# Reordering the row pieces of a DFT stage so that rows loaded from DRAM lie beside a chain of small operations and its exponentials

## Chip, core, metric

One NeuronCore of one Trainium2 chip runs the whole program. The metric is device time in microseconds (us) of one execution; the time before is the median of three runs. Times on the page and in the trace are in us from the first instruction, unless ns is written.

Names of engines: PE is TensorE (matrix multiply), PEld its weight loads, DVE is VectorE, ACT is ScalarE, POOL is GpSimd, and SP is the engine that issues the DMAs.

## What is computed

The input is `x` of shape (8, 256, 96, 96): eight images of 256 channels. Two layers, each with a group norm ahead of it and a residual around it:

```python
# layer 0: attention over channels in the Fourier domain
q_f = fft2(pconv(gn(x), w1, b1)); k_f = fft2(pconv(gn(x), w2, b2)); v_f = fft2(pconv(gn(x), w3, b3))
q_f = l2_normalize(q_f); k_f = l2_normalize(k_f)             # over all 9216 positions, 8 heads of 32 channels
attn = einsum('bhcn,bhdn->bhcd', q_f, k_f) * temperature
attn = softmax(real(attn)) + 1j * softmax(imag(attn))
x = x + pconv(abs(ifft2(einsum('bhcd,bhdn->bhcn', attn, v_f))), w_out)
# layer 1: linear attention with softplus features
x = x + L1_conv(gn(x), Wq, bq, Wk, bk, Wv, bv)
```

The kernel never transforms the images for q and k: it needs only channel sums of products (`pair_sums`), from which the 32 x 32 logits of each head follow. The values need one more linear map of every image along its rows and columns. That map is "R" of the change: `rotate(b)` multiplies each row of image b, transposed, by a table of its own.

## The kernel before: the stage that the change touches

For each image b the program runs, one after the other: `attention(b)` woven with `rotate(b)`; the rest of `rotate(b)`; `images(b)`; `layer1(b)`; `output(b)`. The channel sums of the next image are woven into the last three.

`rotate(b)` is a generator of 48 steps. A step handles two rows h and h+1 of the image. For rows that are not spilled it transposes them on PE (four 128 x 128 transposes), and ACT copies the result from PSUM into a ring of six slots, `xT`. Rows 16 to 79 but for 48 are "spilled" in images 1 to 7: `pair_sums` has already written them, transposed, to DRAM (`xtd`), and a DMA of 192 KB brings the two rows into the slot instead. Two steps later the rows are multiplied by their table (`tm`), and the product is copied from PSUM to the image `y`.

```python
def spilled(h):
    return b > 0 and PR * T0 <= h < H - PR * T0 and h != H // 2       # 16 <= h < 80, not 48

pieces = [TR * i for i in (15, 14, 3, 4, 0, 5, 6, 1, 7, 8, 13, 9, 10, 2, 11, 12)]   # TR = 6 rows
order = [h + r for h in pieces for r in range(0, TR, 2)]
...
def fetch(i):
    if i < len(order) and spilled(order[i]):
        xts[i] = xT[:, i % NX]                                        # NX = 6
        ...
        nc.sync.dma_start(out=xts[i][0:W, :, 0:C], in_=rows.rearrange("(r w) n -> w r n", w=W))

def step(h, due, xt=None, on_scalar=False):
    if h is not None:
        pt = ps_tile(f"xr_{b}_{h}")                                   # ps: a pool of five PSUM banks
    if due is not None:
        g, gt, tm = due
        pu = ps_tile(f"y_{b}_{g}")
    for r in range(2):
        for k in range(KC):
            if h is not None and h + r:
                nc.tensor.transpose(pt[...], x_of(b)[:, k, o:o + W], ident)            # L661
            if due is not None and g + r:
                nc.tensor.matmul(pu[...], lhsT=gt[...], rhs=tm[:, g % TR + r, :], ...)  # L664
    if due is not None:
        nc.vector.tensor_copy(ys[:, :, g + r:g + 2], src[:, :, W, r:2])                 # L669
        (nc.scalar.copy if on_scalar else nc.vector.tensor_copy)(y[...], src[...])      # L670
    if h is not None:
        nc.scalar.copy(xt[0:W, r:2, 0:C], pt[...])                                      # L674

tms = [load_r(g) for g in pieces[0:3]]            # tables, three buffers, one load of 218 KB for a piece
...
for i, h in enumerate(order):
    if i % (TR // 2) == 2 and i > 2 and pieces:
        tms.append(load_r(pieces.pop(0)))
    ...
    due = pending.pop(0) if len(pending) == 2 else None
    step(None if spilled(h) else h, due, xts[i],
         due is not None and spilled(due[0]) and spilled(h) and i % 2)
    pending.append((h, xts.pop(i), tm))
    fetch(i + 3)
    yield
```

`attention(b)` is a chain of small operations for the 32 x 32 logits. Each `yield n` in it lets n steps of `rotate` run before the chain goes on:

```python
... group norm ...                       # yields 2, 1
... scr, cov ...                ; yield 4
qkm matmuls                     ; yield 1        # after step 6
covT, scaling by rstd           ; yield 2        # after step 7
cw products, m = 0, 1           ; yield 1, 1     # after steps 9, 10
cw2 matmuls, ACT scales them    ; yield 2        # after step 11
lg logits, m = 0, 1             ; yield 1, 1     # after steps 13, 14
ssk, square roots, reciprocal   ; yield 1        # after step 15
ssq, square roots, reciprocal   ; yield 4        # after step 16
ls = lg * rk * rq, maximum, two Exp on ACT (L556), division, sbd   ; yield 10   # after step 20
at matmuls (L566)               ; yield 3        # after step 30
mz matmuls (L580)               ; yield 1, 1     # after steps 33, 34
```

PE and POOL keep this program order here; the order on DVE and ACT is chosen by the scheduler when the program is built, earlier code first where both are ready.

Of the kernel before, what the change touches and what calls it, by code (L numbers as in the profile page):

```python
# [62 lines left out]
TR = 6  # L63
# [9 lines left out]
def two_layer_kernel(ctx: ExitStack, tc: tile.TileContext, x, w1t, b1, w2t, b2, w3, b3, wot, temp,  # L73
# [26 lines left out]
    def x_of(b):  # L100
        return arenas[b % 2]

    def y_of(b):
        return arenas[1 - b % 2]

    def x_col(h):

        if h < H // 2:
            t, r = divmod(h, PR)
        elif h == H // 2:  # L110
            t, r = 0, 2 * PR - 1
        else:
            t = (H - h) // PR
            r = 2 * PR - 1 - (H - h) % PR
        return ((NT - 1 - t) * ROWS + r) * W
# [14 lines left out]
    def ps_tile(name):  # L130
        return psum.tile([P, 512], F32, tag="ps", name=name)
# [147 lines left out]
    def window(h, n, back):  # L279

        v = (rb if back else rt)[h:h + n, 0 if back else 1:]
        return bass.AP(v.tensor, v.offset, [[1, W], [2 * W, n], [1, W]])

    def turned(c, h, w):

        return xtd[c, (h - PR * T0) * W + w:]
# [36 lines left out]
    def image(t):  # L323
        return t.rearrange("p k (h w) -> p k h w", w=W)
# [282 lines left out]
    def rotate(b):  # L607

        y = image(y_of(b))
        ys = one.tile([P, KC, H + 1], F32, tag="ys", name=f"ys_{b}")  # L610

        def spilled(h):

            return b > 0 and PR * T0 <= h < H - PR * T0 and h != H // 2

        def load_r(h):
            tm = three.tile([P, TR * (W + 1)], F32, tag="tm", name=f"tm_{b}_{h}")[0:W].rearrange("p (r w) -> p r w", r=TR)
            turned = H // 2 <= h < H - PR * T0
            if b > turned:
                nc.sync.dma_start(out=tm, in_=rx[h // TR])  # L620
                return tm
            lo = 0
            while lo < TR:
                back = h + lo > H // 2 and spilled(h + lo)
                hi = lo + 2
                while hi < TR and back == (h + hi > H // 2 and spilled(h + hi)):
                    hi += 2
                nc.sync.dma_start(out=tm[:, lo:hi, 0:W], in_=window(h + lo, hi - lo, back))
                lo = hi
            nc.gpsimd.tensor_copy(tm[:, :, W:W + 1], csn[0:W, 2, h:h + TR].unsqueeze(2))  # L630
            if b == turned:
                nc.sync.dma_start(out=rx[h // TR], in_=tm)
            return tm


        pieces = [TR * i for i in (15, 14, 3, 4, 0, 5, 6, 1, 7, 8, 13, 9, 10, 2, 11, 12)]
        order = [h + r for h in pieces for r in range(0, TR, 2)]
        xts = {}

        def fetch(i):  # L640

            if i < len(order) and spilled(order[i]):
                xts[i] = xT[:, i % NX]
                h = order[i]
                c = h > H // 2
                rows = turned(c, H - h - 1 if c else h, 0)[0:2 * W]
# [5 lines that stand above are left out]
                pt = ps_tile(f"xr_{b}_{h}")  # L652
            if due is not None:
                g, gt, tm = due
                back = g > H // 2 and spilled(g)
# [4 lines that stand above are left out]
                        o = x_col(h + r)  # L660
                        nc.tensor.transpose(pt[0:W, r * C + k * P:r * C + (k + 1) * P], x_of(b)[:, k, o:o + W], ident)  # L661
                    if due is not None and g + r:
                        o = (r * KC + k) * (W + 1)
                        nc.tensor.matmul(pu[:, o:o + W + 1], lhsT=gt[0:W, 1 - r if back else r, k * P:(k + 1) * P], rhs=tm[:, g % TR + r, :],  # L664
                                         start=True, stop=True)
            if due is not None:
                src = pu[:, 0:2 * KC * (W + 1)].rearrange("p (r k w) -> p k w r", r=2, k=KC)
                r = 0 if g else 1
                nc.vector.tensor_copy(ys[:, :, g + r:g + 2], src[:, :, W, r:2])  # L669
                (nc.scalar.copy if on_scalar else nc.vector.tensor_copy)(  # L670
                    y[:, :, :, g + r:g + 2], src[:, :, 0:W, r:2] if back else src[:, :, W - 1::-1, r:2])
            if h is not None:
                r = 0 if h else 1
                nc.scalar.copy(xt[0:W, r:2, 0:C], pt[0:W, r * C:2 * C].rearrange("p (r n) -> p r n", n=C))  # L674

        tms = [load_r(g) for g in pieces[0:3]]
        pieces = pieces[3:]
        pending = []
        for i, h in enumerate(order):
            if i % (TR // 2) == 0:  # L680
                tm = tms.pop(0)
            if i % (TR // 2) == 2 and i > 2 and pieces:
                tms.append(load_r(pieces.pop(0)))
            if i == len(order) - TR:
                o = x_col(0)
                nc.gpsimd.tensor_copy(y[:, :, :, 0], x_of(b)[:, :, o:o + W])
                nc.gpsimd.memset(ys[:, :, 0:1], 0.0)
            if not spilled(h):
                xts[i] = xT[:, i % NX]
            due = pending.pop(0) if len(pending) == 2 else None  # L690
            step(None if spilled(h) else h, due, xts[i], due is not None and spilled(due[0]) and spilled(h) and i % 2)
            pending.append((h, xts.pop(i), tm))
            fetch(i + 3)
            yield
        for p in pending:
            step(None, p)
        y0[b] = ys
# [333 lines left out]
    with tc.manual_schedule(engines={mybir.EngineType.DVE, mybir.EngineType.Pool}):  # L1031
        for _ in range(NT):
            next(sums)
        tables()
        finish(sums)
    turns = rotate(0)
    for b in range(B):
        with tc.manual_schedule(engines={mybir.EngineType.PE, mybir.EngineType.Pool}):
            weave(attention(b), turns)
            finish(turns)  # L1040
            b3_part(b)
        sums = pair_sums(b + 1) if b + 1 < B else iter(())
        weave(images(b), sums)
        weave(layer1(b), sums)
        with tc.manual_schedule(engines={mybir.EngineType.PE, mybir.EngineType.DVE, mybir.EngineType.Pool, mybir.EngineType.SP,
                                         mybir.EngineType.Activation}):
            weave(output(b, *l1.pop(b)), sums)
            if b + 1 < B:
                turns = rotate(b + 1)
                finish(sums)  # L1050
# [50 lines left out]
```

## Time and profile before

| what | before |
|---|---|
| time, median of 3 runs | 2730.31 us |
| lowest, highest run | 2726.63, 2734.25 us |
| span of the profiled execution, mean granted PE clock | 2728.5 us, 0.984 |
| products of rows (L664, PE), in image 2 of eight | 380 matmuls, median 275 ns |
| copies of products, L670: on DVE, on ACT | 321 of 548 ns, 63 of 491 ns (medians) |
| copies of transposed rows, L674 (ACT) | 167, median 583 ns |
| loads of spilled rows, `xT<-xtd` | 217 of 192 KB |
| loads of tables, `tm<-rx` | 106 of 218.2 KB |

How to read it: a matrix multiply in 32-bit floats is counted as two PE instructions. Busy shares are averages over stages with different limits, so the questions are when PE stands still within this stage, what it waits for, and at what clock it goes on. A stage here is the stretch from the first transpose of `rotate(b)` to the first matmul of `images(b)`.

### The profile page before, as it was taken

What the parts mean: (1) busy time and instruction counts of PE and PEld (TensorE: products, weight loads), DVE (VectorE), ACT (ScalarE), POOL (GpSimd) and SP (SyncE); (2) the same over time, 40 slices, a digit from 0 to 9 for tenths busy, and PEclk for the clock granted to TensorE, in tenths of its full rate; (3) what the DMA queues carried; (4) which work ended last, traced back from release to release, by engine and by line L of the source; (5) the groups of instructions that cost most, each with busy time, mean ns of one, the idle gap of its engine ahead of it and who ended that gap; (6) DMA issues with size and microseconds to landing.
All of it is one profiled execution on the core that took longest, in us unless ns stands there. A gap on an engine that the chain in (4) does not pass through costs nothing. (4 is left out here: it accounts for less than half of the span.)

```text
span 2728.5 us, 47701 instructions
## 1 busy us (share of the span) xinstructions
PE 2682.3 (98%) x17494; PEld 1927.4 (71%) x17494; DVE 1922.3 (70%) x4099; ACT 1355.1 (50%) x2160; POOL 890.1 (33%) x1335
## 2 busy tenths in 40 slices
PE   9999999999999999999999999999999999999988
PEld 8965679656786567955679567785677856778546
DVE  6678576785768757587676876768757596576766
ACT  3455653455535565255642556425474355643554
POOL 6133431334313344033440443404424134241311
PEclk9999998999999999999999999999999999999997
DMA  5220265302652026520275203642036410373003
GB/s 175 67 65 12 70 215 166 85 18 65 203 182 78 10 78 233 149 64 10 82 235 143 70 20 99 223 134 58 30 104 225 123 53 32 102 231 100 1 7 139
DMA packets 243183, 283.59 MB, mean 104 GB/s; under 512 B 37380, under 2 KB 231240, under 8 KB 242952
## 3 DMA queue, kind: packets, MB, share of 16 engines
q1 hardware_dynamic: 242008, 280.22, 33.2%
q8 instruction: 140, 2.29, 0.4%
q14 instruction: 91, 0.75, 0.1%
q10 hardware_dynamic: 944, 0.34, 0.0%
HBM read 156.76 MB, written 123.72 MB: 103 GB/s over the span
## 5 line engine op out<-in xcount | busy, mean ns | idle before, releaser
L746 PE MATMUL z<-arena,mz 128*128 128x384 f32 (+2 forms) x2400 | 597.6, 480 | 0.0
L758 PE MATMUL po<-e,wo 128*128 128x384 f32 x1536 | 529.7, 486 | 0.2 <-ACT e L793 0.2
L792 POOL TENSOR_TENSOR e<-e 128x768 f32<-128x768 f32 x192 | 348.6, 1815 | 554.1 <-ACT e L791 550.5
L746 PEld LDWEIGHTS z<-arena,mz 128*128 128x128 f32 (+1 forms) x2400 | 326.3, 164 | 243.5 <-issue 44.5
L337 PE MATMUL acc<-xT 128*128 128x256 f32 (+1 forms) x2368 | 447.4, 330 | 2.5 <-POOL xT L417 1.8
L664 PE MATMUL y<-tm,xT 96*128 96x97 f32 x3040 | 421.8, 277 | 9.2 <-ACT xT L674 6.4
L758 PEld LDWEIGHTS po<-e,wo 128*128 128x128 f32 x1536 | 289.4, 190 | 197.7 <-DVE arena L760 1.2
L664 PEld LDWEIGHTS y<-tm,xT 96*128 96x128 f32 x3040 | 411.6, 198 | 24.8 <-issue 12.9
L787 DVE TENSOR_TENSOR e<-z,xT 128x768 f32<-128x768 f32 x384 | 365.8, 953 | 86.0 <-PE z L746 85.2
L290 DVE BATCH_NORM_STATS2 st<-arena 128x6 f32<-128x384 f32 x768 | 410.2, 553 | 13.2 <-DMA arena<-in_x_dram 2.8
L337 PEld LDWEIGHTS acc<-xT 128*128 128x128 f32 x2368 | 382.0, 191 | 44.8 <-DVE xT L419 5.9
L791 ACT ACTIVATE e<-e 128x1536 f32<-128x1536 f32 x192 | 284.5, 1482 | 91.4 <-DVE e L787 89.9
L793 ACT ACTIVATE e<-e 128x768 f32<-128x768 f32 x192 | 161.9, 843 | 337.2 <-POOL e L792 334.7
L405 ACT ACTIVATE xt<-eoT,pw 128x512 f32<-128x512 f32 x296 | 203.6, 688 | 181.0 <-PE eoT L404 169.3
L417 POOL TENSOR_TENSOR xT<-xt 128x256 f32<-128x256 f32 x352 | 256.9, 747 | 70.8 <-ACT xt L405 69.3
L760 DVE TENSOR_TENSOR arena<-arena,po 128x384 f32<-128x384 f32 x384 | 211.0, 551 | 90.6 <-PE po L758 67.6
L669 DVE COPY ys<-y 128x4 f32<-128x4 f32 (+1 forms) x384 | 62.0, 161 | 182.6 <-PE y L664 181.8
L670 DVE COPY arena<-y 128x384 f32<-128x384 f32 (+1 forms) x321 | 175.2, 546 | 1.4 <-issue 1.4
L674 ACT COPY xT<-xr 96x512 f32<-96x512 f32 (+1 forms) x167 | 94.5, 572 | 156.9 <-PE xr L661 143.0
L381 POOL COPY back<-arena 128x256 f32<-128x256 f32 (+1 forms) x230 | 86.0, 380 | 265.1 <-PE eoT L404 253.9
L1005 POOL TENSOR_TENSOR arena<-arena,po 128x384 f32<-128x384 f32 x96 | 96.4, 1004 | 232.4 <-ACT po L1004 229.5
L661 PE MATMUL xr<-ident,arena 128*96 128x128 f32 x652 | 171.4, 281 | 0.0
(235 smaller groups left out, 3311.1 us busy)
## 6 DMA issues: line engine op xcount, KB each, us to landing
out_dram<-arena SPq DMA_DIRECT2D x184, 384.0 KB
arena<-in_x_dram SPq DMA_DIRECT2D x182, 384.0 KB
xtd<-xt SPq DMA_DIRECT2D x336, 128.0 KB
xT<-xtd SPq DMA_DIRECT2D x217, 192.0 KB
tm<-rx SPq DMA_DIRECT2D x106, 218.2 KB
rx<-tm SPq DMA_DIRECT2D x16, 218.2 KB
tm<-rt SPq DMA_DIRECT2D x16, 216.0 KB
arena<-in_x_dram SPq DMA_DIRECT2D x8, 288.0 KB
```

Source lines behind the costliest of these rows:

```text
L290: nc.vector.bn_stats(out=st[:, k, c, :], in_=x_of(b)[:, k, c * CH:(c + 1) * CH])
L337: mm = nc.tensor.matmul(acc[c][:, m * C:m * C + (KC - m) * P], lhsT=t[0:np_, c, m * P:(m + 1) * P], rhs=t[0:np_, c, m * P:C], start=(first ...
L405: nc.scalar.activation(both, pt, AF.Copy, scale=pw[:, j:j + 1])
L417: on_pool(eo[:, c], both[:, 0], both[:, 1])
L664: nc.tensor.matmul(pu[:, o:o + W + 1], lhsT=gt[0:W, 1 - r if back else r, k * P:(k + 1) * P], rhs=tm[:, g % TR + r, :], start=True, stop=True)
L670: (nc.scalar.copy if on_scalar else nc.vector.tensor_copy)(y[:, :, :, g + r:g + 2], src[:, :, 0:W, r:2] if back else src[:, :, W - 1::-1, ...
L746: mm = nc.tensor.matmul(out[:, o:o + n * W], lhsT=columns(mz, k, c, j), rhs=y[:, k, h * W:(h + n) * W], start=(k == 0 and o == 0), stop=(k ...
L758: nc.tensor.matmul(po[:, 0:CH], lhsT=wo[:, k, m * P:(m + 1) * P], rhs=e[:, k, :], start=(k == 0), stop=(k == KC - 1))
L760: nc.vector.tensor_add(x[:, m, n], x[:, m, n], po[:, 0:CH])
L787: nc.vector.tensor_add(e[:, 2 * c:2 * c + 2, :].rearrange("p t (q h) -> p t q h", h=H), pz[:, 0:CH].rearrange("p (q h) -> p q h", h=H).uns ...
L791: nc.scalar.activation(e, e, AF.Square)
L792: nc.gpsimd.tensor_add(e[:, 0:2, :], e[:, 0:2, :], e[:, 2:4, :])
```

## The change

The pieces of six rows are taken in another order. Rows that come from DRAM need no transposes and no copy by ACT, so steps with such rows are short on PE and leave ACT alone. The change puts twelve such steps in a row (6 to 17) beside the densest part of the chain, six more (21 to 26) beside the exponentials, and spreads the others, which had been bunched at the end, over the rest. It also keeps ACT from copying products in steps 24 to 27.

```diff
-        pieces = [TR * i for i in (15, 14, 3, 4, 0, 5, 6, 1, 7, 8, 13, 9, 10, 2, 11, 12)]
+        pieces = [TR * i for i in (15, 14, 3, 4, 5, 6, 0, 7, 9, 1, 8, 10, 2, 11, 13, 12)]
...
-            step(None if spilled(h) else h, due, xts[i], due is not None and spilled(due[0]) and spilled(h) and i % 2)
+            step(None if spilled(h) else h, due, xts[i], due is not None and spilled(due[0]) and spilled(h) and i % 2 and not 24 <= i < 28)
```

## Prediction

> **What bounds the kernel now.** I read the page first. Its engine totals name the only candidate; the slices below them say that the clock is not always full.
>
> ```profile
> PE 2682.3 (98%) x17494; PEld 1927.4 (71%) x17494; DVE 1922.3 (70%) x4099; ACT 1355.1 (50%) x2160; POOL 890.1 (33%) x1335
> ```
>
> PE has something in its pipe for 98% of the span, so a change of order that adds and removes no matmul can gain in two ways only: PE stands still less, or runs less at a reduced clock. Next I asked what PE waits for.
>
> ```profile
> PE y L664 <- ACT xT L674: 6.4, 8, 0.9
> ...
> PE y L664 <- DMA xT<-xtd: 2.1, 2, 1.4
> ```
>
> Both top lines of this stage are small: 6.4 us in eight waits on ACT's copy of transposed rows, 2.1 us in two waits for a row from DRAM. Then I cut the span into the seven stages of images 1 to 7, each from its first transpose to the first matmul of `images` (columns: length; busy time and instructions of PE, PEld, DVE, ACT, POOL; granted clock; DMA share; GB/s).
>
> ```profile
> 419.07:492.92 73.85, 71.55 (x537) 67.94 (x535) 39.43 (x136) 19.44 (x40) 1.91 (x11) 0.86 0.52 145
> 763.23:826.06 62.83, 61.98 (x538) 58.52 (x536) 39.42 (x136) 19.47 (x40) 0.20 (x2) 1.00 0.50 146
> 1094.67:1162.67 68.00, 67.09 (x537) 63.47 (x535) 39.44 (x136) 19.49 (x40) 0.39 (x4) 0.92 0.47 136
> 1434.28:1497.34 63.06, 62.12 (x538) 58.52 (x536) 39.34 (x136) 19.48 (x40) 0.20 (x2) 1.00 0.52 145
> 1765.79:1829.42 63.63, 62.13 (x538) 58.53 (x536) 39.34 (x136) 19.46 (x40) 0.28 (x4) 1.00 0.51 144
> 2098.03:2166.05 68.02, 67.17 (x537) 63.48 (x535) 39.42 (x136) 19.47 (x40) 0.20 (x2) 0.92 0.48 136
> 2434.53:2497.30 62.77, 61.92 (x537) 58.46 (x535) 39.34 (x136) 19.45 (x40) 0.30 (x4) 1.00 0.52 147
> ```
>
> The same 537 or 538 instructions take 62.8 us at clock 1.00 and 68.0 or 73.9 us at 0.92 and 0.86. Stages that differ in nothing but clock differ by 5 to 11 us. Where does the clock fall? I took the pieces of lower clock from the trace's record of it and put beside them the same work of image 2 (last line).
>
> ```profile
> 455.80:469.50 13.70, 13.70 (x69) 13.68 (x69) 4.87 (x17) 1.24 (x3) 0.45 (x3) 0.50 0.56 149
> 486.50:496.80 10.30, 10.30 (x79) 9.26 (x81) 2.95 (x13) 0.48 (x1) 0.16 (x2) 0.50 0.05 15
> 1131.70:1141.90 10.20, 10.20 (x51) 10.18 (x51) 3.95 (x14) 0.58 (x1) 0.00 (x0) 0.50 0.42 123
> 2135.20:2145.40 10.20, 10.20 (x51) 10.18 (x50) 3.94 (x14) 0.58 (x1) 0.00 (x0) 0.50 0.41 121
> 798.90:809.10 10.20, 10.20 (x93) 10.07 (x91) 6.80 (x24) 1.75 (x3) 0.00 (x0) 1.00 0.62 187
> ```
>
> At clock 0.50 a stretch of 10.2 us holds 51 matmuls, at 1.00 it holds 93. Each drop lies just behind a wait of PE in this stage: 455.8 is 36.7 us into image 1's stage, 1131.7 is 37.0 into image 3's, 2135.2 is 37.2 into image 6's, and in all seven stages PE stands still for 0.85 us at 35.2. The drop at 486.5 follows the wait of 1.45 us for a row from DRAM in image 1. The 0.85 us is explained by the timelines of ACT and PE in image 2:
>
> ```profile
> 795.32 0.58 ACT L674 COPY xT<-xr 96x512 f32<-96x512 f32 x1 [0.65 <-DMA xT<-xtd]
> 795.92 1.28 ACT L556 ACT_TABLE_LOAD   x1
> 797.22 0.32 ACT L556 ACTIVATE l<-l,nmax 128x32 f32<-128x32 f32 x1
> 797.44 0.19 ACT L556 ACTIVATION_READ_ACCUMULATOR l<-l,nmax 128x1 f32 x1
> 797.53 0.30 ACT L556 ACTIVATE l<-l,nmax 128x32 f32<-128x32 f32 x1
> 797.75 0.19 ACT L556 ACTIVATION_READ_ACCUMULATOR l<-l,nmax 128x1 f32 x1
> 797.84 0.56 ACT L674 COPY xT<-xr 96x512 f32<-96x512 f32 x1
> ```
> ```profile
> 798.46 2.03 PE L664 MATMUL y<-tm,xT 96*128 96x97 f32 x16 [0.85 <-ACT xT L674]
> ```
>
> The copy for step 23's rows stands behind the table load and the two Exp in ACT's queue and ends at 798.40; PE, which wants these rows two steps later, goes on at 798.46.
>
> [...] the trace has exactly 1283 ns for all eight loads before the Exp. [...] the trace shows 0.50 and 1.00 only, the halves 3.4, 6.8, 10.2 or 13.7 us long but for the last. [...] a gap of 0.85 us was followed by half clock in three stages of seven. [...]
>
> **The change part by part.** Write S for a step with rows from DRAM, N for one with rows transposed on PE. From the piece lists, steps 0 to 47 were 6N 6S 3N 6S 3N 3S 1N 3S 2N 6S 2N 7S, and become 6N 12S 3N 6S 4N 5S 2N 5S 2N 3S: 31 S and 17 N either way. In the PE timeline an S step follows the last by 0.89 us, an N step by 1.23 us. PE's work is the same, moved about.
>
> *The exponentials.* They stand behind step 20 in program order. Steps 21, 22, 23 were N and become S; with 24 to 26 that is six steps in which PE needs nothing of ACT. The last N before them is 20, whose copy comes ahead of the Exp; the next is 27. Steps 12 to 14 gain 3 x 0.34 us, 18 to 20 lose it, so step 20 ends where it did (about 30.0 us into the stage), and step 27 begins at 30.0 + 6 x 0.89 = 35.4. In image 2 ACT was through with the Exp at 797.94 - 763.23 = 34.7, though the copies of 21 and 22 came first; now it has none there. So the wait goes in seven images: 7 x 0.85 = **5.95 us**.
>
> *The clock.* With the wait the drops behind it should go. Measured against image 7's 62.77: image 3 has 5.23 us over it, image 6 5.25, image 1 11.08 (two drops and the DRAM wait). Sum **21.6 us**.
>
> *The tail.* Seven S steps in a row at the end took 192 KB each in 0.89 us, plus a 218 KB table in three steps. By the DMA landings in the trace, a row fetch of image 2 landed 2.4 us after issue when the queue was quiet and 3.3 to 4.2 us in the tail; margins before PE's use fell to 0.14 to 0.8 us, and images 1 and 5 missed by 1.45 and 0.65. Afterwards there are runs of five and three S in the last 17 steps, with N between; a row fetched in such a run lands with 1 us or more to spare. Image 5 gains **0.65 us**; image 4's 0.29 over the base is left as noise. Image 1's 1.45 is counted in its 11.08.
>
> *ACT's copies of products.* The condition (odd step, it and the one two before both S) held at 9, 11, 17, 19, 35, 37, 43, 45, 47; now at 9, 11, 13, 15, 17, 23, 33, 35, 41, 47, with 25 barred. Seven copies of about 0.55 us leave DVE and seven of 0.49 join ACT, neither on the path while PSUM banks come free in time.
>
> The most that can be gained is 5.95 + 21.6 + 0.65 = 28.2 us.
>
> **What takes part of it back: the rivals.**
>
> *DMA waits move instead of going.* Rows 24 to 26 now lie in a run of six S without chain matmuls. The fetch for a row may start when its slot is free, about 4.5 us (five S steps) before use. The loads of steps 18 to 23 are 6 x 192 + 2 x 218 KB in 3 x 1.23 + 3 x 0.89 = 6.4 us, about 250 GB/s; in the old tail steps 38 to 43 asked for the same in 6.0 us, or 265 GB/s, and just failed in two images of seven. I expect 0.5 to 1.5 us of margin in images 2 to 7. Image 1 is worse: its tables for pieces 8 to 13 come in small packets and are written back, on the same queue, behind a copy by POOL. I give it 60% for a wait near 1 us and half that for a drop worth 5 us: about 2 us expected. If all seven images missed by 0.5 us, some with drops, 10 to 20 us would be lost and the time would be about 2720.
>
> *DVE or the chain becomes the bound.* In steps 21 to 26 DVE has six times 0.16 + 0.55 us and about 3.0 us of the softmax's small operations, 7.3 less one ACT copy, in 5.4 us of PE. It falls behind by 1.4 us or so. Five PSUM banks of `ps` let it lag by about 3.5 us in S steps, and N steps 27 to 30 give it back. Ahead, cw2 on ACT ends 1.1 us after its matmuls; the steps that hide it before the logits shrink from 2.5 to 1.8 us. Enough, with little over: a wait here in all seven images has perhaps one chance in eight and would cost up to what the change saves (2725 to 2735).
>
> *The drops have another cause.* Images 2, 4, 5 and 7 had the same wait and no drop; if drops come at random, 6 us or so remain and the time is about 2722. Against it: all three drops begin within 2 us of that wait.
>
> **Range and chances.** 2730.3 - 28.2 = 2702; plus 2 for image 1, 1 to 2 for a chance drop elsewhere[...], and 1 for the second rival's share gives **2707 us**. The runs before spread over 7.6 us, some one or two drops of 5 us, so I add that on both sides and more above: 2698 to 2723. Over 2% faster needs less than 2675.7, more than every excess of this stage together: 0.01. Over 2% slower needs 2785, or 8 us lost in every image: 0.02. Within 2%: 0.97.
>
> **What would show it.** Right: no wait of L664 on L674 behind the Exp in images 1 to 7; stages of 62.0 us at clock 1.00; 70 ACT copies at L670. A wait at 0.5 us or more on `xT<-xtd` at steps 24 to 28 shows the first rival; a wait of PE on DVE or ACT near the logits or from step 25 on the second; half clock in stages without a wait the third. I'd be wrong if the stages shorten and the total does not, for then the drops have gone to other stages.

## Result, and the profile after

The changed kernel takes 2706.72 us (median of four runs, 2702.92 to 2712.83); the kernel before takes 2728.47 us in its four runs. The ratio is 0.9919 with a 95% interval of 0.9894 to 0.9944. Both were run again with the experiments: 2705.68 us (11 runs) against 2723.92 us (25 runs), ratio 0.9932, interval 0.9913 to 0.9950. So the gain is some 18 to 22 us, 0.7 to 0.8%, and the predicted 2707 us holds. How it is made up holds less well. One of experiment 2's 20 runs, over 1.5% above the fastest of its kernel, counts as slow, and the ratio there leaves it out.

The page of the changed kernel still has PE at 98%, with the same number of instructions:

```profile
span 2700.8 us, 47703 instructions
...
PE 2659.0 (98%) x17494; PEld 1905.6 (71%) x17494; DVE 1916.3 (71%) x4092; ACT 1357.6 (50%) x2167; POOL 889.3 (33%) x1335
```

PE's busy time fell by 23.3 us (2682.3 to 2659.0) without one matmul fewer: the matmuls got faster, not fewer. The seven stages of images 1 to 7 show where (stretch and length; busy time of PE, PEld, DVE, ACT, POOL; granted clock; DMA share; GB/s):

```profile
421.01:484.91 63.90, 62.42 (x537) 58.50 (x535) 38.49 (x135) 19.92 (x41) 2.09 (x12) 1.00 0.60 167
753.41:815.51 62.10, 61.95 (x537) 58.42 (x535) 38.48 (x135) 19.94 (x41) 0.20 (x2) 1.00 0.54 147
1083.98:1146.25 62.27, 62.12 (x537) 58.50 (x535) 38.47 (x135) 19.94 (x41) 0.34 (x4) 1.00 0.54 148
1414.74:1476.84 62.10, 61.95 (x537) 58.43 (x535) 38.48 (x135) 19.96 (x41) 0.20 (x2) 1.00 0.53 147
1745.44:1808.25 62.81, 62.40 (x537) 58.58 (x536) 38.47 (x135) 19.94 (x41) 0.20 (x2) 1.00 0.53 147
2076.71:2138.82 62.11, 61.96 (x538) 58.43 (x536) 38.46 (x135) 19.94 (x41) 0.20 (x2) 1.00 0.53 148
2407.55:2469.65 62.10, 61.95 (x537) 58.43 (x535) 38.48 (x135) 19.94 (x41) 0.32 (x4) 1.00 0.54 149
```

All seven are at clock 1.00; their sum is 437.39 us, where it was 462.16. Of the span's 27.7 us, 24.8 lie here. The first stretches of `images` in images 1 and 3 give 4.9 us (143.57 and 144.90 us became 141.78 and 141.77): half clock had run on into the one for 3.9 us, and a piece of 6.8 us had begun at the start of the other. A later start of image 0's stage takes 1.9 back. Nothing else moved by more than 0.3 us.

In the totals of PE's waits, the line for ACT's copy of transposed rows (6.4 us before) has left the top of the list; the DRAM rows have not (from line 637 of the kernel on, every line stands one further down than before, so L664 is now L665):

```profile
PE y L665 <- DMA xT<-xtd: 1.6, 2, 1.3
```

And ACT's timeline near the exponentials of image 2, with the copy of step 20's rows ahead of the table load:

```profile
783.48 0.58 ACT L675 COPY xT<-xr 96x512 f32<-96x512 f32 x1 [0.25 <-PE xr L662]
784.08 1.28 ACT L556 ACT_TABLE_LOAD   x1
786.76 0.32 ACT L556 ACTIVATE l<-l,nmax 128x32 f32<-128x32 f32 x1 [1.39 <-DVE nmax L553]
786.98 0.19 ACT L556 ACTIVATION_READ_ACCUMULATOR l<-l,nmax 128x1 f32 x1
787.08 0.31 ACT L556 ACTIVATE l<-l,nmax 128x32 f32<-128x32 f32 x1
787.29 0.19 ACT L556 ACTIVATION_READ_ACCUMULATOR l<-l,nmax 128x1 f32 x1
787.38 0.47 ACT L671 COPY arena<-y 128x384 f32<-128x384 f32 x1
790.08 0.58 ACT L675 COPY xT<-xr 96x512 f32<-96x512 f32 x1 [2.23 <-PE xr L662]
```

The Exp now wait for DVE's maximum (1.39 us) and PE does not wait for them; the next copy of transposed rows comes 2.2 us after ACT went idle.

### The profile page after: what moved, and what is told of

It is laid out like the page before. It is cut to its first block, busy times and chain, and to the rows that moved or that the text cites. A ratio compares the mean times of both kernels' runs of the same rounds, so it can differ in the third digit from the quotient of the medians.

```text
span 2700.8 us, 47703 instructions
## 1 busy us (share of the span) xinstructions
PE 2659.0 (98%) x17494; PEld 1905.6 (71%) x17494; DVE 1916.3 (71%) x4092; ACT 1357.6 (50%) x2167; POOL 889.3 (33%) x1335
## 5 line engine op out<-in xcount | busy, mean ns | idle before, releaser
L665 PE MATMUL y<-tm,xT 96*128 96x97 f32 x3040 | 406.4, 270 | 3.6 <-DMA xT<-xtd 1.6
L665 PEld LDWEIGHTS y<-tm,xT 96*128 96x128 f32 x3040 | 395.5, 192 | 20.5 <-issue 12.1
L419 DVE SCALAR_TENSOR_TENSOR xT<-eoT,pw,xt 128x256 f32<-128x256 f32 x240 | 107.2, 478 | 87.9 <-ACT xt L405 87.8
L1002 DVE TENSOR_TENSOR arena<-arena,o 128x384 f32<-128x384 f32 x288 | 142.4, 549 | 38.3 <-PE o L997 38.2
```

## Experiments

Theory: the wait of 0.85 us behind the exponentials brings half clock with it, and wait and clock together are the gain. Rivals: the even spread of the DRAM rows is the gain; or half clock comes by chance with any shift of work. Unless another kernel is named, "changed" is 2705.68 us. S and N are steps with rows from DRAM and with transposes, as in the prediction; half clock is a granted clock of 0.50, and a piece is a stretch of it. Experiments 1 to 4, 5 to 8 and 9 to 12 ran on three chips, on which the kernel before took 2726.04, 2723.92 and 2725.79 us (53, 25 and 12 runs), so a difference across these sets is good to about 2 us. Profiles are of one execution each.

**1. The exponentials alone**

```diff
-pieces (15, 14, 3, 4, 0, 5, 6, 1, 7, 8, 13, 9, 10, 2, 11, 12)   # before
+pieces (15, 14, 3, 4, 0, 5, 1, 6, 7, 8, 13, 9, 10, 2, 11, 12)   # and ACT barred in steps 24 to 27
```

> Only pieces 6 and 1 change places in the old order, so that steps 18 to 20 transpose and steps 21 to 26 take rows from DRAM; the dense part of the chain and the bunched tail stay as they were. Theory (the 0.85 us wait behind the exponentials brings half clock with it, and the two together are nearly all of the gain): the wait is gone in images 1 to 7, no half clock some 37 us into a stage, a time within 4 us of the changed kernel (2704 to 2713), the rest being the tail's waits on rows from DRAM in images 1 and 5. Rival (the gain comes from the whole spread of the DRAM rows): under half of the gain, 2718 or more.

Measured: 2715.46 us (17 runs) against 2726.04 for before (53 runs), ratio 0.9964, interval 0.9950 to 0.9979. The wait behind the exponentials is gone, one of 0.42 us has come at step 19, ahead of them, and images 2 to 7 took 62.4 to 62.8 us at full clock, as the theory wants. All the same the time is 2.5 us over its range, and the gain, 10.6 us, is a little over half of the whole: too little for the theory as put, too much for its rival. Image 1 has the rest:

```profile
418.32:490.65 72.33, 67.05 (x537) 62.84 (x535) 39.13 (x136) 19.35 (x40) 1.91 (x11) 0.94 0.55 147
```
```profile
PE y L665 <- DMA xT<-xtd: 5.1, 4, 2.4
```

Three of the four late DRAM rows are image 1's (1.80, 0.69, 2.38 us), and half clock came with the last for 13.7 us. The bunch at the end costs more than the 1.45 us that I read off the kernel before.

**2. The spread of the last 24 steps alone**

```diff
-pieces (15, 14, 3, 4, 0, 5, 6, 1, 7, 8, 13, 9, 10, 2, 11, 12)
+pieces (15, 14, 3, 4, 0, 5, 6, 1, 7, 9, 8, 10, 2, 11, 13, 12)
```

> The first 24 steps in the old order, the last 24 spread as in the change; steps 21 to 23 still transpose at the exponentials. Theory: the 0.85 us waits stay in all seven images, with half clock behind some of them; the time stays within 5 us of the kernel before (2723 to 2732). Rival (spread of the DRAM rows): half of the gain or more, 2717 or less.

The last 24 steps are close to the change's and not the same: they begin with pieces 7, 9, 8 where the change has 9, 1, 8.

Measured: 2729.76 us (20 runs, 2712 to 2754), ratio 1.0019, interval 0.9997 to 1.0040. The wait is unchanged:

```profile
PE y L665 <- ACT xT L675: 6.4, 8, 0.9
```

So the spread by itself gains nothing, though image 1's stage in this profile is 65.5 us long where before had 73.85. Something takes it back. In this profile half clock came behind one of the seven waits only, in image 5, but it stayed for 17.1 us, longer than any in the stages of the kernel before:

```profile
1748.25:1819.17 70.92, 70.07 (x537) 66.20 (x535) 38.89 (x135) 19.94 (x41) 0.21 (x2) 0.88 0.46 129
1785.70:1802.80 17.10, 17.10 (x77) 16.52 (x76) 5.31 (x20) 2.04 (x4) 0.00 (x0) 0.50 0.38 108
```

Experiments 9 and 10 come back to that length.

**3 and 4. The wait put back, and work in its place**

```diff
-                nc.scalar.copy(xt[0:W, r:2, 0:C], pt[...])
+                for _ in range(1 + again):            # again = 2 at step 20 of images 1 to 7, else 0
+                    nc.scalar.copy(xt[0:W, r:2, 0:C], pt[...])
```

> The changed kernel, but ACT copies the rows of step 20 three times in a row in images 1 to 7 (two copies of 0.58 us too many), so that PE waits for them again near the exponentials, by 0.8 to 1.0 us; no PE work is added. Theory (a wait of PE near 0.9 us brings half clock in some images): 7 x 0.9 = 6 us of waits plus two to four pieces of half clock at 5 us, 2718 to 2734 in all. Rival (half clock belonged to the old order's other work there): the waits alone, 2711 to 2715, and no half clock in the stages.

For the work, step 20's four transposes are made two more times ahead of the step, in place of the copies:

```diff
+            for r in again * (0, 1):                  # again = 2 at step 20 of images 1 to 7, else 0
+                for k in range(KC):
+                    nc.tensor.transpose(pt[...], x_of(b)[:, k, o:o + W], ident)
```

> The changed kernel with eight transposes too many at step 20 of images 1 to 7, 0.9 us of PE work each, in place of a wait. Theory: the work costs its own length, 7 x 0.9 = 6 us, 2710 to 2716, and no half clock comes. Rival [...]: 2718 to 2734 as with the wait.

Measured: 2716.92 us with the wait (13 runs, 2708.5 to 2726.7), 2714.65 with the work (12 runs, 2712.3 to 2721.9). The wait came to 0.81 us in all seven images, and half clock behind it to one, image 6:

```profile
2083.76:2151.78 68.02, 67.06 (x537) 63.37 (x536) 38.76 (x135) 21.25 (x43) 0.20 (x2) 0.92 0.47 135
```

Its 68.02 us are 4.9 over the 63.15 of four other images with the same wait and full clock (the fifth took 63.21), and half of its 10.2 us at half clock is 5.1. The run as a whole lies between theory and rival, under the theory's range, 11.2 us over the changed kernel (9.1 if each is measured from the kernel before on its own chip). Besides 7 x 0.81 = 5.7 us of waits and the piece of image 6, its profile has a piece of 3.4 us behind image 1's late row and one at the start of `images` in images 2 and 5, so these sums do not account for the time to a microsecond. The work costs its length, as the theory has it, and its time lies in the theory's range: six of the seven stages are 0.9 to 1.5 us longer than 62.10 and at full clock. Image 1 has a piece of 3.4 us behind its late row here too, and two more stand at the start of `images`, in images 2 and 6. The two times differ by less than their spread, so this pair of runs does not show that a wait of 0.8 us costs more than work of that length. Such a wait is a risk of half clock, then, not its sure cause.

**5. The changed kernel again**

> The changed kernel itself, unaltered, for a base with more runs than the four it has, beside the other kernels of this set. Both theories: 2704 to 2711, with no half clock or one or two pieces in the profile.

Measured: 2705.68 us (11 runs, 2702.1 to 2714.1), no half clock in the seven stages.

**6. The old order, one copy moved to DVE**

```diff
-                nc.scalar.copy(xt[0:W, r:2, 0:C], pt[...])
+                (nc.vector.tensor_copy if b > 0 and i == 23 else nc.scalar.copy)(xt[0:W, r:2, 0:C], pt[...])
```

> The kernel before, with its own order; only the copy of step 23's transposed rows goes to DVE in images 1 to 7, so that it does not stand behind the exponentials. DRAM rows stay as bunched as they were. Theory (the wait behind the exponentials is what brings most half clock): the 0.85 us waits are gone or under 0.3 us, no half clock 37 us into a stage, 2707 to 2715. Rival (half clock belongs to the old order as a whole: its bunched rows, its DMA waits, its mix of steps): only the waits' own 6 us are won, 2718 to 2724.

Measured: 2714.15 us (14 runs) against 2723.92, ratio 0.9956, interval 0.9940 to 0.9973: 9.8 us from one copy in each of seven images. The time is in the theory's range; the wait went from 0.85 to 0.42 us, not under 0.3 as expected. That is 3.0 us, and 6.8 are left, most likely for the clock: images 2 to 7 stayed at 1.00 in this profile. Image 1 did not, at its DRAM rows:

```profile
419.57:490.39 70.82, 67.19 (x538) 62.86 (x536) 39.74 (x137) 18.98 (x39) 1.90 (x11) 0.93 0.56 150
760.63:822.96 62.33, 61.91 (x538) 58.45 (x536) 39.74 (x137) 18.98 (x39) 0.20 (x2) 1.00 0.52 147
```

So the exponentials are worth about 10 us, by either way of clearing them. What is left is image 1: against experiment 5's profile its stage is 7.1 us longer (70.82 for 63.73 us), and the other six together take the same (374.3 and 374.5 us).

**7. The wait doubled**

As in experiment 3 with `again = 4`.

> The changed kernel with ACT copying step 20's rows five times in images 1 to 7 (four copies too many), so that PE waits about 2.0 us each time near the exponentials, where 0.8 us was tried before. Theory (the longer the wait, the likelier half clock): 7 x 2.0 = 14 us of waits plus four or more pieces of half clock at 5 us: 2740 to 2765. Rival (waits of this size cost their own length): 2718 to 2725.

Measured: 2758.93 us (4 runs, 2753.4 to 2765.1). The wait is 2.04 us, and half clock came with it in seven images of seven, between its end and 1.1 us later; image 4:

```profile
1472.39 1.97 PE L665 MATMUL y<-tm,xT 96*128 96x97 f32 x12 [2.04 <-ACT xT L676]
```
```profile
1439.23:1508.48 69.25, 67.06 (x537) 63.37 (x535) 38.82 (x135) 22.37 (x45) 0.20 (x2) 0.93 0.47 132
1473.40:1483.70 10.30, 10.30 (x53) 10.30 (x52) 4.24 (x16) 2.03 (x7) 0.00 (x0) 0.50 0.23 65
```

69.25 - 62.10 = 7.15 us, which is the wait and half of 10.24 us. Over the run: 7 x 2.04 = 14.3 us of waits, and five pieces of 10.24 and two of 13.65, 78.5 us, of which half is 39.2; together 53.5, against 53.3 between the medians. Here the rival (a wait costs its own length) is off by a factor of nearly four.

**8. Without the bar on ACT**

```diff
-... and i % 2 and not 24 <= i < 28)
+... and i % 2)
```

> The changed kernel without its second line: ACT copies the product of step 25 again, seven copies more on ACT and seven fewer on DVE. Theory (a lone copy on ACT there is behind the exponentials but PSUM has banks to spare): within 2 us of the changed kernel, no new wait of PE over 0.2 us. Rival (the copy holds its PSUM bank until PE wants it): a wait of PE near step 28 or 30 in every image, 5 us or more.

Measured: 2707.07 us (5 runs, 2703.6 to 2711.1), and no new wait that comes in every image. The second line of the change does nothing that can be seen. In the old order it would have barred nothing: steps 25 and 27 copied no product on ACT there.

**9 and 10. The doubled wait, with the transposing steps sooner and later**

Both start from experiment 7, in which the steps from 21 on run 6 S, 4 N, 5 S.

```diff
-pieces (15, 14, 3, 4, 5, 6, 0, 7, 9, 1, 8, 10, 2, 11, 13, 12)
+pieces (15, 14, 3, 4, 5, 6, 0, 7, 1, 9, 8, 10, 2, 11, 13, 12)   # sooner: 3 S, 3 N, 3 S, 1 N
+pieces (15, 14, 3, 4, 5, 6, 0, 7, 9, 10, 1, 8, 2, 11, 13, 12)   # later: 9 S, 4 N
```

The theory of this pair is that the steps with transposes end half clock and those with DRAM rows do not, so that its length goes with the place of the former; in experiment 7, with the transposing steps at 27 to 30, the pieces lasted 10.2 or 13.7 us.

> The kernel with the doubled wait of 2.0 us near step 22, whose seven pieces of half clock lasted 10.2 or 13.7 us, with one change: pieces 9 and 1 change places, so that the transposing steps come at 24 to 26 rather than 27 to 29. Theory [...]: the pieces of half clock last 3.4 or 6.8 us, 7 x 1.7 to 7 x 3.4 us less than before, 2735 to 2748. Rival (the length of half clock is set by the wait alone): lengths of 10.2 us and more, 2753 to 2765.

> As the last, but the transposing steps come later: pieces 10 and 1 change places with 8 behind them, so that steps 21 to 29 all have DRAM rows. Theory (as before): the pieces of half clock last 13.7 or 17.1 us, 7 x 1.7 to 7 x 3.4 us more, 2766 to 2784. Rival: lengths of 10.2 and 13.7 us as with the order of the change, 2753 to 2765.

Measured: 2741.94 us sooner (5 runs, 2736.0 to 2747.1), 2781.42 later (3 runs, 2777.3 to 2781.6). The waits are the same 2.04 us in all; the pieces at half clock last 3.4 us (three images) or 6.8 (four) sooner, 17.1 (six) or 13.7 (one) later. Image 4 of the sooner kernel:

```profile
1430.10:1497.72 67.62, 65.43 (x538) 61.74 (x536) 37.87 (x133) 23.36 (x47) 0.20 (x2) 0.95 0.49 135
1464.90:1471.70 6.80, 6.80 (x37) 6.80 (x36) 2.50 (x11) 1.98 (x6) 0.00 (x0) 0.50 0.39 105
```

Image 4 of the later kernel:

```profile
1451.98:1524.51 72.53, 70.34 (x537) 66.64 (x535) 39.48 (x136) 21.87 (x44) 0.20 (x2) 0.88 0.45 127
1486.50:1503.50 17.00, 17.00 (x84) 16.98 (x83) 6.29 (x24) 2.43 (x8) 0.00 (x0) 0.50 0.35 98
```

PE is busy for the whole of the low stretch in both, by its row. Yet steps with DRAM rows alone do not bring the clock back, and steps with transposes do: in all 21 images of these two kernels and of experiment 7 the clock returned between 2.9 and 6.3 us after the first N of a run of three or four began. Here theory and rival are told apart without overlap. It also bears on experiment 2: there the transposing steps behind the exponentials had moved from 27 and 31, 32 to 30 and 36, 37, and the one piece lasted 17.1 us where it lasts 10.2 or 13.7 in the old order. That longer pieces are the reason why the spread alone gained nothing is not shown: it rests on one profile, of an execution of 2715.66 us, 14 us faster than the median of that kernel.

**11. The dense part undone**

```diff
-pieces (15, 14, 3, 4, 5, 6, 0, 7, 9, 1, 8, 10, 2, 11, 13, 12)
+pieces (15, 14, 3, 4, 0, 5, 1, 6, 7, 8, 9, 10, 2, 11, 13, 12)
```

> Pieces 15, 14, 3, 4, 0, 5, 1, 6, 7, 8, 9, 10, 2, 11, 13, 12: rows from DRAM at the exponentials as in the change and no bunch at the end, but three transposing steps stay beside the dense part of the chain, so that the rest has a run of eight steps with DRAM rows (28 to 35). Theory (the dense part matters only because chain matmuls give the DMAs time, so that three steps with DRAM rows fit there at no risk): the wait behind the exponentials is gone, and DRAM rows are late by up to 1 us in some of images 2 to 7 near steps 32 to 37 and by more in image 1; 2707 to 2718. Rival (the dense part gains nothing): within 2 us of the changed kernel's 2705.7, no late rows beyond image 1.

Measured: 2709.77 us (5 runs, 2707.9 to 2710.8), inside the theory's range, 4 us over the changed kernel. By the DMA landings, images 2 and 6 had a late row of 0.61 us each, at steps 28 and 43 and not where the theory has them, and image 1 had three (1.97, 0.41 and 0.63 us; the list of waits puts the last, and image 6's, down to DVE). Image 1's stage is 66.30 us long against 63.73 in experiment 5. PE waits 0.42 us at step 19 in six of the seven images and 0.70 in one, where the changed order has 0.15. So putting DRAM rows beside the chain is worth a few us: 2.6 in image 1, where the rest has more room, and some 2 by the shorter wait at step 19.

**12. Two touches more**

```diff
-... and not 24 <= i < 28)
+... and not 24 <= i < 28 and i != 17)
...
-                nc.sync.dma_start(out=rx[h // TR], in_=tm)
+                nc.gpsimd.dma_start(out=rx[h // TR], in_=tm)
```

> The changed kernel with two more touches: ACT copies no product at step 17 (DVE does), and image 1 writes its tables back to DRAM from POOL's queue rather than from the queue of the row loads. Theory: the 0.15 us waits at step 20 go in seven images (1.0 us), and image 1's wait of 1.3 us for a row at step 43 halves at least; 2702 to 2706. Rival (the row is late for the bandwidth that small packets take, not for the queue): image 1's wait stays at 1 us or more; 2704 to 2707.

Measured: 2705.30 us (6 runs, 2703.3 to 2715.2): no gain over 2705.68. Both of the theory's expectations failed, and the rival's wait and time came out. The 0.15 us wait stands in all seven images, so it was not ACT's copy of a product at step 17. By the trace it stands in step 19, not 20, and ends with ACT's copy of step 18's rows (in image 2 the copy ends at 786.18 and PE goes on at 786.23). The matmul that waits uses step 17's rows, which had landed 5 us before; why it waits for that copy was not found. Image 1's late row stands too:

```profile
PE y L665 <- DMA xT<-xtd: 3.1, 3, 1.3
```

The longest is image 1's, 1.31 us where it was 1.30 to 1.33; image 3 had one of 1.28 and image 5 one of 0.56, so the margins of the changed order are thin elsewhere too. In image 1 the queue that issues the write-back is not what makes the row late. That leaves image 1's own traffic, of which the trace of the changed kernel shows 208 GB/s in packets of 785 bytes on average from 45 to 60 us into the stage, against 151 GB/s in packets of 1133 bytes in image 2; that this makes the row late was not tested. No version was found that beats the changed kernel.

## Why the prediction was right, and where not

**The exponentials, 5.95 us.** Right in kind: the wait behind the table load and the Exp is gone in seven images. 0.15 us came in its place, at step 19, so 7 x 0.70 = 4.9 us were won. I had not foreseen that rest.

**The clock, 21.6 us.** Right in kind, and by far the largest term. Between the two profiles the stages gave 24.8 us, of which 5.6 are waits of PE on others (8.2 us down to 2.6), so 19.2 are clock, by difference; the half clock in `images`, which I had not counted, gave 4.9 more. Over many runs the whole gain is 18 us against a kernel before of 2724 to 2726 us, so I estimate the clock's usual part, `images` included, at about 13 us, the 18 less some 5 of waits: the profile that I counted from had more half clock than the typical run. The term was sized from one execution of something that changes from run to run: the mean granted clock of the 25 runs of the kernel before beside experiment 5 was 0.979 to 0.993. Nor did image 1 differ "in nothing but clock": its late row is in its 11.08.

**The tail.** Here a step failed. "A row fetched in such a run lands with 1 us or more to spare" is not so. By the DMA landings in the trace, image 2's rows of steps 41 and 42 had 0.39 and 1.28 us to spare, image 6's 0.93 and 0.16; image 1's row of step 41 came 1.33 us late. So image 1's 1.45 us, which I had put into its 11.08, did not go: it moved to step 43 of the new order, in every profile of the changed order. The half clock behind it did not surely go either: of seven profiles of this order it is absent in four (the first, experiments 5, 7 and 8) and there in three (3, 4 and, for 17.1 us, 12), so that the first profile had none of it was partly luck. What did go are the larger waits of 2.3 to 2.4 us, with 13.7 us of half clock, which the old bunch has once the exponentials are cleared (experiments 1 and 6).

**First rival, moved DMA waits.** It was about half right. Image 1 kept a wait near 1 us, as I gave 60% for, but at step 43, not beside the exponentials. Of images 2 to 7 only image 5 was late by more than 0.3 us, by 0.41 us in the second profile (0.27 in the first). The margins of the rows of steps 24 to 26 in the first profile were 0.39 to 0.84 us in images 2, 4, 6 and 7, at or below the lower end of my 0.5 to 1.5; in images 1, 3 and 5 some were 0.14, the time from landing to matmul that late rows show too, so these had nothing to spare.

**Second rival, DVE or the chain.** It did not come. The largest wait that names DVE in the changed kernel's stages is 0.27 us, in one image of experiment 5's profile, and there a row from DRAM had landed only 0.14 us before PE went on, so it may have been the row.

**Third rival, drops by chance.** I weighed it as either cause or chance. The runs make it a matter of degree: behind waits of 0.4 us half clock came in none of 14 images (experiments 1 and 6), behind 0.81 to 0.85 us in 5 of 21 (before, experiments 2 and 3), at 2.04 us in 21 of 21 (experiments 7, 9 and 10). The length of the wait is not all, though: at waits for DRAM rows it came in 6 of 12 of 1.0 to 1.5 us, in neither of two of 1.8 and 2.0 us (image 1, experiments 1 and 11) and in both of 2.3 and 2.4 us. What else decides was not found.

**The sum.** 2702 plus 4 to 5 us of allowances gave 2707. That it fits to a microsecond is luck, for two errors met in it: the clock's typical part was put too high, and the base of 2730.3 us, too, was some 5 us, one piece of half clock, above the median of many runs.

**How long half clock lasts.** A busy PE did not end it by itself: in images 2 to 7 of experiment 10, steps with DRAM rows alone went on at 0.50 for 10.6 to 13.4 us, with PE busy throughout by the profile, until the transposes began. In image 4 of experiment 7 it cost half of its length: the wait and half of the 10.24 us make 7.16 us, and the stage is 7.15 us longer. What in the transposing steps brings the clock back was not shown.

## What to carry to other kernels

On a kernel bound by PE, a wait of two microseconds cost two to five times its length here, and one of 0.81 to 0.85 us brought half clock in 5 of 21 images, so cut the span into equal stages and compare their clocks before adding up waits. Where a wait can't be avoided, put right behind it the work that brings the clock back, in this kernel the steps with transposes: in images 2 to 7 the same wait of 2.04 us lengthened the stage by 3.9 to 5.6 us with two DRAM steps ahead of the transposes, by 7.2 to 8.8 us with five and by 8.8 to 10.4 us with eight. And size such a term from the times of many runs, since one profile holds one draw of it.

## What the runs showed that I had not expected

- Half clock outlasts its cause by what follows: 3.4 to 6.8, 10.2 to 13.7 or 13.7 to 17.1 us behind one and the same wait of 2.04 us, by where the transposes stood.
- Half clock can come with no wait at all. In the profile before and in those of six experiments (3, 4, 7, 8, 11, 12) a piece of 3.4 or 6.8 us begins within 0.5 us of the first matmul of `images`, with no idle time of PE over 0.15 us in the 5 us ahead of it, behind 24 matmul instructions with one column each that take 1.2 us (L594). It is short, and half of it is 1.7 to 3.4 us. That these narrow matmuls bring it was not tested.
- Thinning out one wait made another longer: with the exponentials cleared in the old order, image 1's late row grew from 1.45 to 2.3 us, presumably since PE, which in the profile before had gone 13.7 us at half clock ahead of the bunched rows, reached them sooner; this was not tested.

The 5 us ahead of such a piece at the start of `images`, and the piece itself, in experiment 8:

```profile
1140.60:1145.60 5.00, 5.00 (x60) 4.97 (x60) 2.72 (x10) 0.49 (x1) 0.10 (x1) 1.00 0.03 8
1145.60:1149.10 3.50, 3.50 (x36) 2.48 (x39) 0.98 (x6) 0.00 (x0) 0.13 (x1) 0.51 0.02 5
```
